# Another order for the seven steps of a nested product, and the plain product read by ScalarE alone

## The chip, the cores and the metric

The kernel runs on one core of one Trainium2 chip. The metric is the device time of one execution in microseconds (us), the median of three runs. All data are float32. TensorE runs a float32 matmul of this kernel as two passes, so one product in the code is two rows in the profile.

## The reference

Eight images x of 512 channels and 32 x 32 = 1024 positions go through two layers.

```python
# layer 0: attention with 8 heads of 64 channels, 1x1 convolutions
q, k, v = conv(x, Wq, bq), conv(x, Wk, bk), conv(x, Wv, bv)
attn = softmax(einsum('bhdn,bhdm->bhnm', q, k) * scale, axis=-1)
x = x + conv(einsum('bhnm,bhdm->bhdn', attn, v), Wp, bp)
# layer 1: non-local block, then a normalization over batch and positions
g_x, theta_x, phi_x = conv(x, g_w), conv(x, theta_w), conv(x, phi_w)   # 256 channels each
f = einsum('bcn,bdn->bcd', theta_x, phi_x) / n
z = conv(einsum('bcd,bdn->bcn', f, g_x), W_w) + x
out = (z - mean(z)) * rsqrt(var(z) + eps) * gamma + beta
```

The change touches the products for q, k and v of layer 0, a 512 x 512 weight times 512 x 1024 data for each image.

## The kernel before

The kernel takes the images one after the other. For image b it runs the attention (scores L578, exponential on ScalarE L581, weighted sum L604), then the products q, v and k of image b+1, then the projection of image b (L340, `pp`), theta and phi (`ptp`), g (`pg`), and the sum z. TensorE, VectorE (`dve`) and SyncE's DMAs are held in the order in which the program lists them.

Large products use a Strassen-Winograd scheme: seven products of quarter size and sums of quarters take the place of eight products. The seven steps are listed in `SEVEN`, each with its weight block, its data block, a chain number, and the quarter that is read out when it is done. Steps with one chain number accumulate in one place, and the sum so far is read out after each of them.

```python
SEVEN = (("11", 0, "11", 0, (("11", True),)), ("s1t1", 3, "t1", 1, (("22", True),)),
         ("s2t2", 4, "t2", 0, (("12", True),)), ("s4", 6, "22", 1, (("12", False),)),
         ("s3t3", 5, "t3", 0, (("22", False),)), ("12", 1, "21", 2, (("11", False),)),
         ("t4", 2, "t4", 0, (("21", True),)))
SIX = (((1, "21", "11"), (6, "22", "12")), ((3, "t1", "22"), (4, "t2", "T6")), ((5, "t3", "T7"), (2, "t4", "21")))
ORDER = (0, 1, 2, 5, 4, 3, 6)
```

For q, k and v of images 1 to 7 the function `six` is used, 21 times in all. Of the seven outer products, one (`plain()`) is done as it is: two halves into one accumulator tile each (L386 for q and k, L383 for v). Each half is read twice, into the temporary `T6` and into the quarter "11" of the result. The function `begin` makes these reads: three of the four by ScalarE (L510 for q and k, L545 for v), the fourth by VectorE (L508, L545). The other six outer products are nested: each is again seven steps. They are done in the three pairs of `SIX`, the two products of a pair side by side (m = 0 and 1), so that one step is two products. The results of a pair go to the quarters 11 and 12, then 22 and T6, then T7 and 21. `ORDER` is the order of the seven steps inside a pair.

A pair has four accumulator tiles from the ring of four tags s0 to s3 (`next_bank`). A tile has two halves of 512 columns. `slots[m]` and `slots[2 + m]` belong to product m. Which tile and half a step uses follows from its chain: chain 0 the first half of `slots[m]`; before the change, chain 1 the first half of `slots[2 + m]`, and chain 2 the second half of `slots[2 + m]`. So along `ORDER` the steps go to the two tiles of a product strictly in turn. The products are L418 (q, k) and L415 (v).

After each step its sum is read from the tile. The first read into a result quarter is a copy by ScalarE (L424), every later one an add by VectorE (L426). The quarters 11 and T6, which already hold the plain product, take adds only, and T7 has a read of its own (`third`: ScalarE L514 for q, VectorE L516 for k and L546 for v).

Between the steps VectorE has other work, which `fills` places. For q it makes the last sums of the next image's data: t4 (L252, from x) behind the plain product, and the four inner sums of t3 and of t4 (L264), one after each of some steps. Behind the second pair ("middle") come the softmax denominators (L644) and their reciprocal (L655).

Of the kernel before, what the change touches and what calls it, by code (L numbers as in the profile page):

```python
# [10 lines left out]
AF = mybir.ActivationFunctionType  # L11
ALU = mybir.AluOpType
# [18 lines left out]
def unshifted(ctx: ExitStack, tc: tile.TileContext, a: dict, out: bass.AP):  # L31
    nc = tc.nc
# [32 lines left out]
    dve = sp = pe  # L65
# [281 lines left out]
                between[n]()  # L347

    SIX = (((1, "21", "11"), (6, "22", "12")), ((3, "t1", "22"), (4, "t2", "T6")), ((5, "t3", "T7"), (2, "t4", "21")))
    ORDER = (0, 1, 2, 5, 4, 3, 6)  # L350

    def six(name, w, data, positions_out, at, begin, third, fills, by_scalar=False):

        fills = dict(fills)
        shape = [P, 4, 256] if positions_out else [P, 2, 512]
        temps = {}

        def to(q):
            if q[0] != "T":
                return at(q)  # L360
            if q not in temps:
                temps[q] = w3.tile(shape, F32, tag="acc", name=f"{q}_{name}")
            return temps[q]

        def piece(q, i, j):
            if positions_out:
                return to(q)[:, j * 2:j * 2 + 2, i * P:(i + 1) * P]
            return to(q)[:, i, j * 256:(j + 1) * 256]

        def add(q, of, engine=None):  # L370
            dve((engine or nc.gpsimd).tensor_tensor(to(q), to(q), to(of), ALU.add))

        def plain():
            d = data["11"]
            for half in range(2):
                ps = next_bank(f"{name}_0_{half}")[:, 0, :]
                if positions_out:
                    ps = ps.rearrange("p (i f) -> p i f", f=256)
                for i in range(2 if positions_out else 1):
                    for k in range(2):  # L380
                        if positions_out:
                            at = (half * 2 + i) * P
                            pe(nc.tensor.matmul(ps[:, i, :], d[:, k, at:at + P], w[:, 0, k, :],  # L383
                                                start=(k == 0 and i == 0), stop=(k == 1), skip_group_check=True))
                        else:
                            pe(nc.tensor.matmul(ps, w[:, 0, k, half * P:(half + 1) * P], d[:, k, :],  # L386
                                                start=(k == 0), stop=(k == 1), skip_group_check=True))
                for q in ("T6", "11"):
                    at_ = to(q)[:, half * 2:half * 2 + 2, :] if positions_out else to(q)[:, half, :]
                    begin(at_, ps, half, half and q == "11")  # L390
            load_w("first")

        plain()
        for one in fills.pop("plain", ()):
            one()
        for n, pair in enumerate(SIX):
            if n == 2:
                add("12", "22")
                add("12", "T6")
                for one in fills.pop("middle", ()):  # L400
                    one()
            slots = [next_bank(f"{name}_in_{n}_{i}") for i in range(4)]
            free[:] = [free[2], free[3], free[0], free[1]]
            begun = set()
            for step, which in enumerate(ORDER):
                _, wi, di, chain, reads = SEVEN[which]
                for m, (outer, of, q) in enumerate(pair):
                    a, d = w.inner(outer)[wi], data[f"inner {of}"][di]
                    ps = slots[m if not chain else 2 + m][:, chain // 2, :256]
                    start = (m, chain) not in begun  # L410
                    begun.add((m, chain))
                    if positions_out:
                        ps = ps.rearrange("p (i f) -> p i f", f=P)
                        for i in range(2):
                            pe(nc.tensor.matmul(ps[:, i, :], d[:, i * P:(i + 1) * P], a, start=start and not i, stop=True,  # L415
                                                skip_group_check=True))
                    else:
                        pe(nc.tensor.matmul(ps, a, d, start=start, stop=True, skip_group_check=True))  # L418
                    for (i, j), is_first in reads:
                        i, j = int(i) - 1, int(j) - 1  # L420
                        if is_first and q == "T7":
                            third(piece(q, i, j), ps, piece("T6", i, j), i)
                        elif is_first and q not in ("11", "T6"):
                            nc.scalar.copy(piece(q, i, j), ps)  # L424
                        else:
                            dve(nc.vector.tensor_tensor(piece(q, i, j), piece(q, i, j), ps, ALU.add))  # L426
                for one in fills.pop((n, step), ()):
                    one()
            load_w()
        assert not fills, fills  # L430
        if by_scalar:
            add("T7", "T6")
        add("22", "T7")
        add("21", "T7")
# [22 lines left out]
    for x_part, w_part in (((0, 1, 0), (w_first[0], 0, 0, 0, 1)), ((1, 2, 0), (w_first[0], 0, 0, 1, 2)),  # L457
# [5 lines left out]
        if w_part:  # L463
            to, m, k, c0, c1 = w_part
            nc.scalar.dma_start(to[:, c0:c1], quarter("WqT", m, k)[:, c0:c1])
    ps = next_bank("warm_ps")[:, 0, :]
# [34 lines left out]
    def heads_of(b, what, w, bias, data, pin=lambda ins: None, steps=None, fills=None, **how):  # L501

        t = mats.tile([P, CC, N], F32, tag=what, name=f"{what}_{b}")

        if fills is not None:
            def begin(to, ps, i, by_vector):
                if by_vector:
                    dve(nc.vector.tensor_scalar(to, ps, bias[:, i:i + 1], 1.0, ALU.add, ALU.mult))  # L508
                else:
                    nc.scalar.activation(to, ps, AF.Identity, bias=bias[:, i:i + 1])  # L510

            def third(to, ps, of, i):
                if what == "q":
                    nc.scalar.activation(to, ps, AF.Identity, bias=steps[:, i:i + 1])  # L514
                else:
                    dve(nc.vector.scalar_tensor_tensor(to, ps, steps[:, i:i + 1], of, ALU.add, ALU.add))  # L516

            six(f"p{what}_{b}", w, data, False, lambda q: t[:, rows(q), cols(q)], begin, third, fills,
                what == "q")
            return t  # L520

        def first(q, ps):
            for m in range(2):
                c = rows(q).start + m
                if how.get("early") and q == "21":
                    nc.vector.tensor_scalar(t[:, c, cols(q)], ps[:, m, :], bias[:, c:c + 1], 1.0, ALU.add, ALU.mult)
                else:
                    nc.scalar.activation(t[:, c, cols(q)], ps[:, m, :], AF.Identity, bias=bias[:, c:c + 1])

        seven(f"p{what}_{b}", w, data, False, first, add_to(t, pin), **how)  # L530

        return t

    def values(b, w, data, fills=None):
        v = mats.tile([P, NB, C], F32, tag="v", name=f"v_{b}")

        def at(q):
            return v[:, (int(q[1]) - 1) * NB // 2:int(q[1]) * NB // 2, (int(q[0]) - 1) * C // 2:int(q[0]) * C // 2]

        def as_v(ps):  # L540
            return ps.rearrange("p h (i f) -> p (h i) f", f=C // 2)

        if fills is not None:
            six(f"pv_{b}", w, data, True, at,
                lambda to, ps, _, by_vector: dve(nc.vector.tensor_copy(to, ps)) if by_vector else nc.scalar.copy(to, ps),  # L545
                lambda to, ps, of, _: dve(nc.vector.tensor_tensor(to, of, ps, ALU.add)), fills)  # L546
            return v
        seven(f"pv_{b}", w, data, True, lambda q, ps: nc.scalar.copy(at(q), as_v(ps)),
              lambda q, ps: dve(nc.vector.tensor_tensor(at(q), at(q), as_v(ps), ALU.add)))
        return v  # L550
# [436 lines left out]
    data = {"11": b11, "21": b21, "22": b22, "t1": t[0], "t2": t[1], "t3": t[2], "t4": t[3], "name": "x_0"}  # L987
    q = heads_of(0, "q", w, bq, data, dve, early=True, by_chunk=True)
# [19 lines left out]
    for b in range(B):  # L1008
# [41 lines left out]
        if not last:  # L1050
            data = nxt["data"]
            t3, t4 = (inner_one_by_one(data, of) for of in ("t3", "t4"))
            q = heads_of(b + 1, "q", weights("WqT"), bq, data, dve, steps=dq, fills={
                "plain": [lambda: more_sums(data, (4,), dve), t3[0]], (0, 0): t3[1:2], (0, 1): t3[2:3],
                (0, 2): t3[3:], (0, 6): t4[:1], (1, 0): t4[1:2], (1, 1): t4[2:3], (1, 2): t4[3:],
                "middle": [lambda: nxt.update(products=normalize(denominators(next_bank(f"den_{b}"))))]})
            products = nxt["products"]
            v = values(b + 1, weights("WvT"), data, fills={(0, 6): products[:2], (1, 6): products[2:]})
# [305 lines left out]
```

## Time and profile before

| | |
|---|---|
| three runs | 2135.11, 2135.65, 2136.66 us; median 2135.65 us |
| the profiled execution | 2135.05 us, span 2133.3 us, mean granted TensorE clock 0.996 |
| TensorE matmul busy | 2093.9 us (98% of the span) |
| VectorE, ScalarE, GpSimd busy | 1409.1, 781.1, 526.0 us |
| q stage of the image at 973.6 us | 25.43 us: PE 23.67, DVE 17.26, ACT 8.20 busy |
| v stage of that image | 22.55 us: PE 22.48, DVE 12.75, ACT 6.33 |
| k stage of that image | 22.09 us: PE 21.82, DVE 13.18, ACT 6.42 |

The stages are seven times in the program, for images 1 to 7. Matmuls are pipelined: a pass of 256 columns has a row of 379 ns, but the next pass starts 216 ns after it. A row of idle time therefore counts from the end of the row before, not from the time at which the next pass could have started. PE stands for the matmuls and PEld for the weight loads ahead of them.

### The profile page before, as it was taken

The numbers are of one execution on the slowest core, as the hardware profiler recorded it, in microseconds if no ns is written. First come the engines' busy times: TensorE is split into PE (matmuls) and PEld (weight loads), VectorE is DVE, ScalarE is ACT, GpSimd is POOL, SyncE is SP. The second block draws the span as 40 slices with busy tenths as digits, with TensorE's granted clock in tenths as the row PEclk, the third lists the DMA queues.
The fourth block names the chain that finished last, engine by engine and source line by source line (L and its number), as shares of the span: only waits on it lengthen the run. The fifth ranks groups of instructions, "written<-read, shape, count | busy, mean of one in ns | idle before, by whom it ended". The sixth has DMA issues, their size and how long they took to land.

```text
span 2133.3 us, 33255 instructions
## 1 busy us (share of the span) xinstructions
PE 2093.9 (98%) x13486; PEld 1173.4 (55%) x13486; DVE 1409.1 (66%) x2072; ACT 781.1 (37%) x1024; POOL 526.0 (25%) x392
## 2 busy tenths in 40 slices
PE   9999999999999999999999999999999999999995
PEld 4535863358733677336773377633775348743462
DVE  6587567765578655786557766577664775556736
ACT  1464204642046410563105631066312652056116
POOL 0012900128001370014601155011550118111000
PEclk9999999999999999999999999999999999999998
DMA  6253533244232432325324253142543235212768
GB/s 227 84 144 77 172 146 111 38 89 142 99 114 41 105 121 99 117 40 139 101 83 121 41 146 122 50 124 42 152 151 139 41 51 165 92 27 40 235 219 318
DMA packets 71728, 243.56 MB, mean 114 GB/s; under 512 B 12688, under 2 KB 21136, under 8 KB 69520
## 3 DMA queue, kind: packets, MB, share of 16 engines
q1 hardware_dynamic: 60640, 215.01, 30.3%
q0 software_dynamic: 9072, 24.78, 9.5%
q8 instruction: 108, 1.77, 0.3%
q10 hardware_dynamic: 1856, 1.56, 0.3%
q14 instruction: 52, 0.43, 0.1%
HBM read 160.45 MB, written 47.32 MB: 97 GB/s over the span
## 4 chain that ended last, share of the span: by engine, by line
PE 94%; DVE 2%; ACT 2%; DMA 1%; issue 0%; SPq 0%; DVEq 0%; ACTq 0%
PE ps L578 21%; PE po L604 21%; PE ptp L340 9%; PE pp L340 7%; PE pv_in L415 6%; PE pk_in L418 6%; PE pq_in L418 5%; PE pg L340 4%; PE pz L340 3%; PE pf L799 2%; PE pp_in_s L297 2%; PE pq L386 1%; PE pq L340 1%; PE pv L383 1%; PE pv L340 1%; PE pk L386 1%
## 5 line engine op out<-in xcount | busy, mean ns | idle before, releaser
L581 ACT ACTIVATE e<-ps 128x1024 f32<-128x1024 f32 x512 | 523.0, 1025 | 422.8 <-PE ps L578 412.1
L587 DVE TENSOR_TENSOR acc<-acc,e 128x1024 f32<-128x1024 f32 x384 | 469.9, 1224 | 103.6 <-ACT e L581 93.7
L578 PE MATMUL ps<-q,k 64*64 64x512 f32 x4096 | 529.3, 589 | 0.0
L604 PE MATMUL po<-e,v 64*64 64x512 f32 x4096 | 528.7, 589 | 0.0
L617 POOL DMA_DIRECT2D fold<-acc x189 | 144.8, 766 | 1359.1 <-DMA fold<-acc 650.4
L604 PEld LDWEIGHTS po<-e,v 64*64 64x64 f32 x4096 | 156.6, 133 | 282.9 <-issue 275.5
L578 PEld LDWEIGHTS ps<-q,k 64*64 64x64 f32 x4096 | 155.5, 133 | 283.4 <-issue 277.3
L842 ACT ACTIVATE g<-pg,gb 128x512 f32<-128x512 f32 x31 | 21.3, 688 | 442.0 <-PE pg L340 441.9
L585 DVE TENSOR_TENSOR acc<-e,e 128x1024 f32<-128x1024 f32 x64 | 78.3, 1224 | 120.8 <-ACT e L581 118.6
L340 PE MATMUL ptp<-w_tp,t_x 128*128 128x256 f32 x512 | 114.4, 379 | 0.0
L340 PEld LDWEIGHTS ptp<-w_tp,t_x 128*128 128x128 f32 x512 | 97.3, 190 | 13.2
L340 PE MATMUL pp<-t_o,w_WpT 128*128 128x512 f32 x208 | 100.8, 592 | 0.0
L340 PE MATMUL ptp<-w_tp,x 128*128 128x256 f32 x384 | 86.8, 379 | 0.0
L340 PEld LDWEIGHTS ptp<-w_tp,x 128*128 128x128 f32 x384 | 73.0, 190 | 13.3 <-issue 3.8
L340 PE MATMUL pp<-o,w_WpT 128*128 128x512 f32 x144 | 67.8, 593 | 1.9 <-DVE o L684 1.9
L424 ACT COPY v<-pv_in 128x256 f32<-128x256 f32 x84 | 31.3, 372 | 100.8 <-PE pv_in L415 33.1
L424 ACT COPY k<-pk_in 128x256 f32<-128x256 f32 x84 | 31.3, 373 | 97.2 <-PE pk_in L418 96.7
L684 POOL TENSOR_TENSOR o<-o,r 128x1024 f32<-128x1024 f32 x28 | 65.3, 2368 | 0.0
L770 DVE TENSOR_TENSOR tp<-tp,ptp 128x1024 f32<-128x1024 f32 x24 | 29.3, 1221 | 51.2 <-PE ptp L340 51.2
L737 DVE SCALAR_TENSOR_TENSOR x<-pp,bp,x 128x512 f32<-128x512 f32 x52 | 37.6, 746 | 35.0 <-PE pp L340 35.0
L418 PE MATMUL pq_in<-i_t_x,w_WqT 128*128 128x256 f32 x224 | 57.1, 382 | 2.9 <-DVE fold L655 2.9
L424 ACT COPY q<-pq_in 128x256 f32<-128x256 f32 x84 | 31.3, 373 | 76.3 <-PE pq_in L418 75.8
(233 smaller groups left out, 2942.1 us busy)
## 6 DMA issues: line engine op xcount, KB each, us to landing
fold<-acc POOLq DMA_DIRECT2D x189, 128.0 KB, 3.1
w_WqT<-kept_WqT SPq DMA_DIRECT2D x21, 896.0 KB, 4.6
w_WvT<-kept_WvT SPq DMA_DIRECT2D x21, 896.0 KB, 4.9
w_WkT<-kept_WkT SPq DMA_DIRECT2D x21, 896.0 KB, 5.3
r<-den_d SPq DMA_DIRECT2D x32, 512.0 KB, 6.9
x<-in_x_dram SPq DMA_DIRECT2D x30, 512.0 KB, 5.8
spill<-x SPq DMA_DIRECT2D x24, 512.0 KB, 4.0
z<-spill SPq DMA_DIRECT2D x24, 512.0 KB, 10.1
```

The costliest lines, as they stand in the source:

```text
L297: pe(nc.tensor.matmul(ps, a[wi], d[di], start=s not in begun, stop=True, skip_group_check=True))
L340: pe(nc.tensor.matmul(to_ps, lhsT(k), rhs(k), start=(s, at) not in begun, stop=(k == nk - 1), skip_group_check=True))
L415: pe(nc.tensor.matmul(ps[:, i, :], d[:, i * P:(i + 1) * P], a, start=start and not i, stop=True, skip_group_check=True))
L418: pe(nc.tensor.matmul(ps, a, d, start=start, stop=True, skip_group_check=True))
L424: nc.scalar.copy(piece(q, i, j), ps)
L578: pe(nc.tensor.matmul(ps[c * P // 2:(c + 1) * P // 2, j, :], k[r, p, keys], q[r, p, h * 512:(h + 1) * 512], start=True, stop=True, skip_gr ...
L581: nc.scalar.activation(e, ps, AF.Exp, scale=SCALE)
L585: nc.vector.tensor_tensor(accs[u], es[u, 0], e, ALU.add)
L587: ins = nc.vector.tensor_tensor(accs[u], accs[u], e, ALU.add)
L604: pe(nc.tensor.matmul(ps[j * D:(j + 1) * D, r, :], v[keys, m, (2 * p + j) * D:(2 * p + j + 1) * D], e[keys, j, :], start=(m == 0), stop=(m ...
L617: nc.gpsimd.dma_start(to, part_of, accum_op=ALU.add)
L684: dve((engine or nc.vector).tensor_tensor(at, at, of, ALU.mult))
```

## The change

There are three parts. First, the order of the seven steps becomes 0, 5, 1, 2, 4, 3, 6, and chain 2 (step 5 alone) moves from the second half of `slots[2 + m]` to the second half of `slots[m]`, the tile of chain 0. Second, the fourth read of the plain product goes from VectorE to ScalarE, so that ScalarE makes all four, in q, k and v. Third, the four inner sums of t3 go, with t4, ahead of everything that VectorE does for the first pair of q, and those of t4 are spread over other steps.

```diff
-    ORDER = (0, 1, 2, 5, 4, 3, 6)
+    ORDER = (0, 5, 1, 2, 4, 3, 6)
...
-                    begin(at_, ps, half, half and q == "11")
+                    begin(at_, ps, half)
...
-                    ps = slots[m if not chain else 2 + m][:, chain // 2, :256]
+                    ps = slots[2 + m if chain == 1 else m][:, chain // 2, :256]
...
-            def begin(to, ps, i, by_vector):
-                if by_vector:
-                    dve(nc.vector.tensor_scalar(to, ps, bias[:, i:i + 1], 1.0, ALU.add, ALU.mult))
-                else:
-                    nc.scalar.activation(to, ps, AF.Identity, bias=bias[:, i:i + 1])
+            def begin(to, ps, i):
+                nc.scalar.activation(to, ps, AF.Identity, bias=bias[:, i:i + 1])
...
-                lambda to, ps, _, by_vector: dve(nc.vector.tensor_copy(to, ps)) if by_vector else nc.scalar.copy(to, ps),
+                lambda to, ps, _: nc.scalar.copy(to, ps),
...
-                "plain": [lambda: more_sums(data, (4,), dve), t3[0]], (0, 0): t3[1:2], (0, 1): t3[2:3],
-                (0, 2): t3[3:], (0, 6): t4[:1], (1, 0): t4[1:2], (1, 1): t4[2:3], (1, 2): t4[3:],
+                "plain": [lambda: more_sums(data, (4,), dve), *t3],
+                (0, 2): t4[:1], (0, 3): t4[1:2], (0, 6): t4[2:3], (1, 0): t4[3:],
```

## The prediction

> **What bounds the kernel.** I read the page first, then TensorE's waits, then the timeline of one image.
>
> ```profile
> span 2133.3 us, 33255 instructions
> ...
> PE 2093.9 (98%) x13486; PEld 1173.4 (55%) x13486; DVE 1409.1 (66%) x2072; ACT 781.1 (37%) x1024; POOL 526.0 (25%) x392
> ...
> PEclk9999999999999999999999999999999999999998
> ```
>
> TensorE is busy for 98% of the span at full clock. The change neither adds nor removes a matmul, so it acts only through the time that TensorE stands still in the 21 calls of `six`. TensorE's waits, in total, count and longest, are there:
>
> ```profile
> PE pq_in L418 <- DVE q L426: 7.7, 7, 1.1
> PE pq_in L418 <- DVE fold L655: 2.9, 7, 0.6
> PE pk_in L418 <- DVE k L508: 1.9, 7, 0.3
> PE pq_in L418 <- DVE q L508: 1.9, 7, 0.3
> ```
>
> Each comes once per image. The timeline of the q stage at 973.6 us shows the first and the last of them:
>
> ```profile
> 978.07 0.75 DVE L508 TENSOR_SCALAR q<-pq,bq 128x512 f32<-128x512 f32 x1 [3.02 <-ACT T_pq L510]
> ...
> 978.87 0.30 PEld L418 LDWEIGHTS pq_in<-i_x,w_WqT 128*128 128x128 f32 x2 [0.67 <-DVE q L508]
> 978.87 0.70 PE L418 MATMUL pq_in<-i_x,w_WqT 128*128 128x256 f32 x2 [0.27 <-DVE q L508]
> ...
> 980.20 0.41 DVE L426 TENSOR_TENSOR q<-q,pq_in 128x256 f32<-128x256 f32 x1
> ...
> 980.67 1.13 PE L418 MATMUL pq_in<-i_x,w_WqT 128*128 128x256 f32 x4 [1.10 <-DVE q L426]
> ```
>
> VectorE stands idle for 3.02 us until ScalarE has read the second plain half, then reads that half itself, makes t4 (1.22) and one inner sum, and only then adds the first product of the pair. TensorE needs that tile again and waits 1.10 us. Two prices follow. From the end of a read to the weight load that it holds up it is 0.055 us (980.617 to 980.672). The weight load, normally hidden under the matmul before, then stands in the open: the matmul's row is 483 ns long instead of 379, so 0.104 us more.
>
> ```profile
> L418 PE MATMUL pk_in<-i_x,w_WkT x112: 379/379/483, 240.9 to 1803.4; 128*128 128x256 f32 x112
> ```
>
> A row ends 0.163 us after its successor could start (379 less 216 ns). So the true loss of a wait is its idle time plus 0.163 plus 0.104, that is idle plus 0.27.
>
> **What goes.** Per image: 1.10 + 0.27 = 1.37 (L426), 0.27 + 0.27 = 0.54 (L508, q), 0.39 + 0.27 = 0.65 (reciprocal L655, in the image at 973.6), 0.54 (L508, k), and 0.33 in v, where one product came 0.06 us late with the weight load in the open. Sum: 3.4 us. All of it should go. VectorE no longer holds the fourth plain read. t4 and the inner sums of t3 take 1.13 + 4 x 0.34 = 2.5 us (each starts that long after the one before it, in the rows above and those of L264 between them) from 975.05, where the last add of the attention ends, so they end at 977.6, before the first sum can be read at 977.78. The reciprocal's bank is needed one step (0.86 us) later, and it was 0.65 late. The inner sums of t4 fit in VectorE's gaps in pairs 0 and 1. The 21 reads that ScalarE takes over cost it 21 x 0.6 us beside TensorE, except for what is charged below.
>
> **What comes.** In the old order the steps of a product take its two tiles in turn: 0 | 1 | 0 | 2 | 0 | 1 | 0 by chains, where 1 and 2 share a tile. In the new order the tiles are A A B A A B A. Twice in each pair a step follows directly on a step in the same tile: 5 after 0, and 4 after 2. The waits in the built program say that this counts: the product of step 5 waits for the read of step 0's product in that tile, by VectorE (m = 0) or ScalarE (m = 1), although it goes to the other half; and 4 waits for the read of 2. The old program also has such waits by whole tile, but with a step between them, so no row of before shows one costing time. What the interval is worth is seen in an undisturbed step:
>
> ```profile
> 995.58 1.03 PE L418 MATMUL pq_in<-t_x,w_WqT 128*128 128x256 f32 x4
> ...
> 996.21 0.42 DVE L426 TENSOR_TENSOR T_pq<-T_pq,pq_in 128x256 f32<-128x256 f32 x1 [2.09 <-PE pq_in L418]
> 996.23 0.84 PEld L418 LDWEIGHTS pq_in<-i_t_x,w_WqT 128*128 128x128 f32 x4
> 996.44 1.03 PE L418 MATMUL pq_in<-i_t_x,w_WqT 128*128 128x256 f32 x4
> ```
>
> A step is four passes, 0.863 us (995.58 to 996.44). The first product's read starts 0.63 after its first pass and lasts 0.42. In the same tile the next step's first matmul can start at 0.63 + 0.42 + 0.055 + 0.104 = 1.21, so 0.35 late. The second product runs 0.43 later throughout and adds nothing, unless its read is the longer one or is held up. Other readers:
>
> ```profile
> L424 ACT COPY q<-pq_in 128x256 f32<-128x256 f32 x84 | 31.3, 373 | 76.3 <-PE pq_in L418 75.8
> L514 ACT ACTIVATE T_pq<-pq_in,dq 128x256 f32<-128x256 f32 x28 | 13.3, 474 | 31.3 <-PE pq_in L418 30.5
> ...
> L516 DVE SCALAR_TENSOR_TENSOR T_pk<-pk_in,dk,T_pk 128x256 f32<-128x256 f32 x28 | 13.5, 484 | 5.4 <-PE pk_in L418 4.8
> ```
>
> The same sum with 0.37 gives 0.30 late, with 0.47 gives 0.40, with 0.48 gives 0.41. In v a step is eight passes of 0.1115, 0.89 us, and the late part is 0.33 for VectorE's 0.42.
>
> Each pair has two such places. In pair 0 (quarters 11 and 12) VectorE reads m = 0, which makes 2 x 0.35 in q and k and 2 x 0.33 in v. At the first place of q and k the fourth plain read is in the way too: it starts 0.59 after the third (977.35), at 977.93, frees ScalarE at 978.52, so the copy of m = 1 ends at 978.89 and its tile is free at 979.05; with the 0.35 the product was due at 978.79. That adds 0.26, and 0.03 in v by the same steps. The sums for q, k and v are 0.96, 0.96 and 0.69. In pair 1 (22 and T6) m = 0 is late by 0.30 for ScalarE's copy, and m = 1 brings it to 0.35 for VectorE's add; two places make 0.70 in q and k, 0.66 in v. In pair 2 (T7 and 21) it is 2 x 0.40 in q, 2 x 0.41 in k and 2 x 0.33 in v.
>
> q 2.46, k 2.48, v 2.01: 7.0 us per image. Less the 3.4 that goes: +3.6 us per image, times 7 images, +25 us. TensorE sets the stages behind (projection, theta, scores), so nothing there gives it back. On the profiled execution that is 2135.05 + 25 = 2160; on the median, 0.6 higher, I say 2161 us.
>
> Bounds of the price: were the weight load hidden after all, 18 x 0.104 x 7 = 13 us less, 2148. Should every third read queue behind another VectorE operation (0.33, the spacing of its adds), 6 x 0.33 x 7 = 14 more, 2175. I stay in the middle because every wait of before, worked out this way, gives its row.
>
> No row of before has a step directly behind another in its tile, so the wait of 5 for 0 rests on the built program. [...]
>
> The 1.10 us waits of before left PEclk at 9. [...]
>
> **Rivals.** *The reads are in time* (faster, 0.03): only the 3.4 us go, 7 x 3.4 = 24, 2112 us. It decides if a read has ended 0.70 us after its product's start (0.863 less 0.16); above it ends at 1.05. *Half the places cost nothing* (same, 0.03): if step 5 does not lose time on step 0, nine places of 0.35 are 3.2 against 3.4, about 2135 us. *Reads queue up* (slower, 0.06): up to 2175, as above; against it, VectorE is busy for 17.26 of the 25.43 us of the q stage and for less of v and k. *The clock drops* (slower, 0.03): the mean of 0.996 stands for 8.5 us lost in the whole span, and only the last slice of PEclk is an 8; a like loss in each of 7 images would give 2161 + 60 = 2221. It would decide if a wait of some tenths of a microsecond in every third of a pair counted for the clock more than the one of 1.10 us did.
>
> **The numbers.** The forecast itself has 0.85 and a range of 2155 to 2167 (0.05 us on each of 18 places, 0.9 us per image, 6 us in all). For 8 in 10 with part of the bounds on the price: 2153 to 2169. A measurement of this kernel tells 0.2%, 4.3 us, from no change. Faster 0.03, same 0.03, slower 0.94.
>
> **What would show it.** Right: TensorE's waits list new entries under pq_in, pv_in and pk_in for L426, L424, L514 (new number L511) and L516, about 18 per image, each with the 483 ns rows; idle of 0.03 to 0.14 us each, since 0.27 of each loss is not idle in the rows; the old L426 and reciprocal waits gone; the image's stages 73.7 us instead of 70.07. Wrong: stages at or under 70 us, or a step 5 that starts 0.86 after step 0.

## The result, and the profile after

The changed kernel takes 2163.28 us (2161.63 to 2164.71 in four runs) against 2135.79 us for the kernel before in the same comparison: 1.0128 times as long, with an interval of 1.0111 to 1.0146. The prediction was 2161 us, with 2153 to 2169 as its range and 0.94 for slower.

The profiled execution took 2162.94 us, its span 2161.2, at a mean granted clock of 0.995. The code of after is a few lines shorter, so lines move: the plain reads are L507 (q, k) and L542 (v), ScalarE's and VectorE's reads in `third` are L511 (q), L513 (k) and L543 (v), the reciprocal is L652, and o of the last image is L681. L414 to L426 keep their numbers. The head of the page:

```profile
span 2161.2 us, 33290 instructions
...
PE 2124.8 (98%) x13486; PEld 1168.8 (54%) x13486; DVE 1402.0 (65%) x2051; ACT 790.3 (37%) x1045; POOL 526.3 (24%) x392
...
PEclk9999999999999999999999999999999999999998
```

TensorE has the same 13486 matmuls, but is "busy" for 30.9 us longer (2124.8 against 2093.9), while the span grew by 27.9. VectorE has 21 instructions fewer and ScalarE 21 more, which is the fourth plain read. So the loss isn't where a reader looks first, in idle time of TensorE; it is inside rows that became longer, and in later starts that lie under the end of the row ahead. TensorE's waits after (total, count, longest; the list shows none under 0.15 us) list only little:

```profile
PE pp L340 <- DVE o L681: 2.1, 1, 2.1
PE pk_in L418 <- DVE T_pk L513: 1.5, 7, 0.2
PE warm_ps L468 <- DVE folds L483: 1.1, 1, 1.1
PE pk_in L418 <- DVE k L426: 1.1, 7, 0.2
PE pq_in L418 <- DVE q L426: 0.8, 5, 0.2
...
```

Under `six` that is 3.4 us, where before had 14.4. The waits of the weight loads show what took their place:

```profile
PEld pq_in L418 <- ACT q L424: 8.2, 21, 0.4
PEld pk_in L418 <- ACT k L424: 8.2, 21, 0.4
PEld pk_in L418 <- DVE T_pk L513: 8.1, 14, 0.6
PEld pq_in L418 <- ACT T_pq L511: 7.5, 14, 0.5
PEld pq_in L418 <- DVE q L426: 7.2, 14, 0.6
...
PEld pv_in L415 <- DVE v L426: 4.1, 14, 0.3
```

Counts of 14 and 21 are two and three in each image, where before had seven of one kind, one in each. Each is some tenths of a microsecond long, and most of it lies beside the end of the matmul ahead, so that TensorE itself shows little idle time. The matmul that waits is lengthened by its own weight load (shortest, median and longest row in ns):

```profile
L418 PE MATMUL pq_in<-x,w_WqT x84: 379/379/483, 190.8 to 1777.4; 128*128 128x256 f32 x84
```

The first pair of q in the image at 984.6 us shows both places of the new order, 5 behind 0 and 4 behind 2 (timeline: start, duration, engine, line; in brackets the idle time ahead and what ended it):

```profile
988.16 1.03 PE L418 MATMUL pq_in<-x,w_WqT 128*128 128x256 f32 x4
...
988.86 0.42 DVE L426 TENSOR_TENSOR q<-q,pq_in 128x256 f32<-128x256 f32 x1 [0.20 <-PE pq_in L418]
988.95 0.68 ACT L507 ACTIVATE q<-pq,bq 128x512 f32<-128x512 f32 x1
...
989.34 0.30 PEld L418 LDWEIGHTS pq_in<-x,w_WqT 128*128 128x128 f32 x2 [0.55 <-DVE q L426]
989.34 1.30 PE L418 MATMUL pq_in<-x,w_WqT 128*128 128x256 f32 x4 [0.15 <-DVE q L426]
989.52 0.38 ACT L424 COPY q<-pq_in 128x256 f32<-128x256 f32 x1
989.94 0.30 PEld L418 LDWEIGHTS pq_in<-x,w_WqT 128*128 128x128 f32 x2 [0.31 <-ACT q L424]
...
992.45 0.30 PEld L418 LDWEIGHTS pq_in<-i_x,w_WqT 128*128 128x128 f32 x2 [0.48 <-DVE q L426]
```

Step 0 starts at 988.16; VectorE reads its first product until 989.28; only then does the weight load of step 5 start, at 989.34. Due 0.863 us behind 988.16, step 5 starts its first pass 0.104 us (the weight load in the open) behind 989.34, so it is 0.42 late, with only 0.15 of that as idle time of PE. The second product is held up by ScalarE's copy, which had to let the fourth plain read (988.95) go first. The old waits are gone: VectorE no longer reads a plain half here, and the reciprocal in the third pair, which held up TensorE before, now ends after 1.76 us without anything of `six` waiting for it:

```profile
1003.12 1.76 DVE L652 RECIPROCAL fold<-den 128x256 f32<-128x256 f32 x1 [0.61 <-PE den L641]
...
1004.24 0.73 PEld L418 LDWEIGHTS pq_in<-t_x,w_WqT 128*128 128x128 f32 x4 [0.53 <-ACT T_pq L511]
```

By stage (window, its length, then busy time of PE, PEld, DVE, ACT, POOL, the granted clock, the DMA share and GB/s), q, v and k of that image:

```profile
984.62:1009.93 25.31, 24.75 (x113) 17.14 (x110) 17.15 (x37) 8.64 (x20) 7.01 (x5) 1.00 0.48 121
1009.93:1034.27 24.34, 23.90 (x185) 22.34 (x184) 12.29 (x30) 6.71 (x17) 21.01 (x9) 1.00 0.69 196
1034.27:1058.44 24.17, 23.52 (x95) 16.71 (x93) 12.63 (x31) 6.89 (x16) 23.60 (x16) 1.00 0.29 93
```

The clock is 1.00 in all three. The time without a matmul row (length less PE busy) is 1.65 us in these three windows, spread over 18 short spells, against 2.10 us in five spells before: it fell while the stages grew. q is 0.12 us shorter than before, v 1.80 and k 2.07 longer. In images 2 to 7 the three together take 73.81 us against 70.06, in image 1 74.92 against 71.33: 6 x 3.75 + 3.6 = 26.1 of the 27.9 us. Between the stages nothing moved (191.33 us from one to the next for most images, and each such stretch the same in both kernels). The rest, 1.9 us, is behind the last stage, and is taken up in the last section.

### The profile page after: what moved, and what is told of

Read it like the earlier page. It is cut to its first block, busy times and chain, and to the rows that moved or that the text cites. A ratio compares the mean times of both kernels' runs of the same rounds, so it can differ in the third digit from the quotient of the medians.

```text
span 2161.2 us, 33290 instructions
## 1 busy us (share of the span) xinstructions
PE 2124.8 (98%) x13486; PEld 1168.8 (54%) x13486; DVE 1402.0 (65%) x2051; ACT 790.3 (37%) x1045; POOL 526.3 (24%) x392
## 4 chain that ended last, share of the span: by engine, by line
PE 94%; DVE 2%; ACT 2%; issue 1%; DMA 1%; DVEq 0%; SPq 0%; ACTq 0%
PE ps L575 20%; PE po L601 20%; PE ptp L340 9%; PE pp L340 7%; PE pv_in L415 6%; PE pq_in L418 6%; PE pk_in L418 6%; PE pg L340 4%; PE pz L340 3%; PE pf L796 2%; PE pp_in_s L297 2%; PE pq L386 1%; PE pq L340 1%; PE pv L383 1%; PE pv L340 1%; PE pk L386 1%
## 5 line engine op out<-in xcount | busy, mean ns | idle before, releaser
L340 PE MATMUL ptp<-w_tp,t_x 128*128 128x256 f32 x512 | 114.4, 379 | 0.0
L340 PEld LDWEIGHTS ptp<-w_tp,t_x 128*128 128x128 f32 x512 | 97.3, 190 | 13.2
L340 PE MATMUL pp<-t_o,w_WpT 128*128 128x512 f32 x208 | 100.8, 592 | 0.0
L340 PE MATMUL ptp<-w_tp,x 128*128 128x256 f32 x384 | 86.8, 379 | 0.0
L426 DVE TENSOR_TENSOR v<-v,pv_in 128x256 f32<-128x256 f32 x112 | 46.6, 422 | 53.9 <-PE pv_in L415 50.6
L340 PEld LDWEIGHTS ptp<-w_tp,x 128*128 128x128 f32 x384 | 73.0, 190 | 13.3 <-issue 3.8
L426 DVE TENSOR_TENSOR k<-k,pk_in 128x256 f32<-128x256 f32 x112 | 46.8, 421 | 49.0 <-PE pk_in L418 47.0
L340 PE MATMUL pp<-o,w_WpT 128*128 128x512 f32 x144 | 69.4, 605 | 2.1 <-DVE o L681 2.1
L681 POOL TENSOR_TENSOR o<-o,r 128x1024 f32<-128x1024 f32 x28 | 65.2, 2368 | 0.0
```

What stands on the lines that cost most here:

```text
L340: pe(nc.tensor.matmul(to_ps, lhsT(k), rhs(k), start=(s, at) not in begun, stop=(k == nk - 1), skip_group_check=True))
L681: dve((engine or nc.vector).tensor_tensor(at, at, of, ALU.mult))
```

## The experiments

Two theories stand against each other. By the prediction's, the time is lost at the places where a step follows another in its tile, some 0.4 us at each, and the read by ScalarE alone is a gain that hides part of it. By the rival, it is lost by what the change moves on VectorE and ScalarE (the fourth read, the early sums), or by the other sequence of the steps as such, and the shared tile costs little. A place is a step that directly follows another in its tile. A stage is the time from the first plain product of q to the first product of the projection; its times are those of images 2 to 7 in the profiled execution. Run times are medians of four runs with their range, and the bracket behind a ratio is its 95% interval. The names e1 to g1 are used again further down.

**The order alone, on the kernel before (e1).**

```diff
-    ORDER = (0, 1, 2, 5, 4, 3, 6)
+    ORDER = (0, 5, 1, 2, 4, 3, 6)
...
-                    ps = slots[m if not chain else 2 + m][:, chain // 2, :256]
+                    ps = slots[2 + m if chain == 1 else m][:, chain // 2, :256]
```

> The new order and the new place of chain 2 alone; the fourth plain read stays with VectorE and the early sums of x stay where they were. One image's stage (first plain product of q to first product of the projection) was 70.06 us before and 73.81 after; without any loss on TensorE it would be 66.6. Theory (a step directly behind a step in the same tile waits for that step's read): the 18 places per image cost what they cost after, and the first of each stage costs more, since VectorE's plain read and the sums stand ahead of the read that step 5 now waits for: about 10.7 us of loss, a stage of 77.4 us, 2187 us in all. Rival 1 (the loss comes from ScalarE, which has four plain reads ahead of its copies): about the time of before, 2136 us, or less. Rival 2 (5 behind 0 costs nothing, since it goes to the other half): 4 behind 2 alone, a stage of 70 us, 2136 us.

Measured: 2194.02 us (2191.32 to 2196.90), 1.0269 [1.0252, 1.0287] of before. The stage takes 77.44 us in images 2, 3 and 5 as worked out, but 78.8 to 79.1 in images 4, 6 and 7. TensorE's waits show what the old order had hidden:

```profile
PE pq_in L418 <- DVE q L426: 17.5, 7, 2.5
PE pk_in L418 <- DVE k L426: 7.2, 7, 1.0
PE pv_in L415 <- DVE v L426: 5.9, 7, 0.8
```

With step 5 directly behind step 0, TensorE waits 2.5 us in every q for the first add of the pair, which on VectorE is queued behind the fourth plain read, t4 and an inner sum. Before, the same add came 1.10 us too late; a step of 0.86 us in the other tile no longer lies ahead of the wait, nor the 0.54 us by which that step was itself held up: 1.10 + 0.86 + 0.54 = 2.50. The order by itself costs more than the whole change does. The 7 us above the expectation are those three images (in image 4 the granted clock was 0.50 for a while, last section), and the part behind the last stage, 320.79 us instead of 317.54, with a wait of 3.41 us for o and 5.40 us for the eight passes behind it, which before took 3.70. The mean granted clock of the span is 0.993, against 0.996 before.

**The change with the old order (e2).** The converse: after, with both lines above undone.

> The other two parts alone: all four plain reads on ScalarE and the early sums, in the old order and the old tiles, where no step follows another in its tile. Theory: the waits for VectorE's plain read go, what stays per image is 0.65 (reciprocal), 0.34 in q and in k (the fourth read on ScalarE frees its tile late) and 0.1 in v: 1.4 us of loss, a stage of 68.1 us, 2122 us in all. Rival 1 (ScalarE's four reads make the loss): well above before, toward 2163 us.

Measured: 2121.95 us (2121.61 to 2122.28), 0.9934 [0.9918, 0.9951]; stage 68.05 us. This is faster than before by 14 us, which is 7 times the 2.0 us by which the stage became shorter. Of TensorE's waits in `six` one is left, the reciprocal:

```profile
PE pq_in L418 <- DVE fold L652: 2.9, 7, 0.6
```

**The new steps, tiles in turn (e3).** After, with step 5 second as in the change, but with an order that goes to the two tiles in turn (A B A B A B A).

```diff
-    ORDER = (0, 5, 1, 2, 4, 3, 6)
+    ORDER = (0, 5, 2, 1, 4, 3, 6)
...
-                    ps = slots[2 + m if chain == 1 else m][:, chain // 2, :256]
+                    ps = slots[m if not chain else 2 + m][:, chain // 2, :256]
```

> The order 0, 5, 2, 1, 4, 3, 6 with chain 2 in its old tile: step 5 comes second as after the change, but the tiles alternate as before. The other two parts as after. Theory: no place of the same tile, so as with the old order: a stage of 68.1 us, 2122 us. Rival 3 (it is the early step 5 as such that costs, its add on VectorE into a quarter just written): near 2163 us.

Measured: 2121.68 us (2121.44 to 2122.79), 0.9934 [0.9917, 0.9950]; stage 68.05 us, the same as with the old order (q, v and k of image 4, columns as above):

```profile
967.80:991.65 23.85, 23.40 (x113) 17.75 (x110) 16.75 (x37) 8.63 (x20) 7.01 (x5) 1.00 0.47 127
991.65:1013.95 22.30, 22.30 (x186) 21.87 (x184) 12.20 (x30) 6.72 (x17) 20.98 (x9) 1.00 0.73 215
1013.95:1035.84 21.89, 21.83 (x94) 17.40 (x93) 12.45 (x31) 6.89 (x16) 21.40 (x15) 1.00 0.31 103
```

Against the old order the steps 1 and 5 have changed places, and it makes no difference. So it isn't the early step 5 that costs, but two steps in one tile one after the other.

**Four places instead of two (e5).** As the last one, but with an order whose tiles are A A B B B A A.

```diff
-    ORDER = (0, 5, 1, 2, 4, 3, 6)
+    ORDER = (0, 2, 1, 5, 3, 4, 6)
...
-                    ps = slots[2 + m if chain == 1 else m][:, chain // 2, :256]
+                    ps = slots[m if not chain else 2 + m][:, chain // 2, :256]
```

> The order 0, 2, 1, 5, 3, 4, 6 with chain 2 in its old tile, the other two parts as after: four places per pair instead of two (2 behind 0, 5 behind 1, 3 behind 5, 6 behind 4), none of them 5 behind 0 or 4 behind 2. Theory: 36 places per image at 0.30 to 0.41, 13.7 us of loss with the fourth read's share, a stage of 80.4 us, 2208 us. Rival 3 (only the early step 5 costs) gives 2122 us. Rival 2 (only places in the same half cost): three of these four places are in the same half or follow one, so 5 behind 1 and 3 behind 5 are free and about 2165 us come out.

Measured: 2207.72 us (2207.21 to 2210.75), 1.034 [1.0323, 1.0357]; stage 80.29 us, but 80.64 in images 4 and 7, where one read of v came late. Image 4:

```profile
1003.83:1031.30 27.47, 26.40 (x112) 16.17 (x109) 17.29 (x37) 8.65 (x20) 7.01 (x5) 1.00 0.47 118
1031.30:1058.14 26.84, 25.84 (x186) 22.95 (x184) 12.40 (x30) 6.72 (x17) 20.99 (x9) 1.00 0.58 171
1058.14:1084.47 26.33, 25.17 (x95) 15.76 (x94) 12.80 (x31) 6.88 (x16) 24.17 (x16) 1.00 0.25 85
```

With none, 18 and 36 places in an image the stage takes 68.05, 73.81 and 80.29 us. It is a dose: twice the places, about twice the time. Of the four places two are in the same half of the tile (2 behind 0, 6 behind 4) and two go to the other half (5 behind 1, 3 behind 5). In the first pair of q of image 4 those to the other half are 0.42 and 0.35 us late, 6 behind 4 is 0.35 late. So the other half is no protection, which settles rival 2.

**The new order with the old tiles (f1).** After, with only the tile of chain 2 undone: A B B A A B A, again two places in a pair, at other steps.

```diff
-                    ps = slots[2 + m if chain == 1 else m][:, chain // 2, :256]
+                    ps = slots[m if not chain else 2 + m][:, chain // 2, :256]
```

> As after, but chain 2 stays in the second half of its old tile, so along 0, 5, 1, 2, 4, 3, 6 the tiles run A B B A A B A: again two places per pair, 1 behind 5 in place of 5 behind 0, and the second tile is needed one step earlier. Theory: 18 places as after, and the waits that the late use of the second tile had removed come back (0.65 behind the reciprocal, 0.34 in q and in k, 0.1 in v, partly inside the places): 8.2 us of loss per image, a stage of 74.9 us, 2169.5 us in all. Rival (the half or the place of step 5 in the tile of step 0 makes the loss): 2136 us or less.

Measured: 2172.96 us (2171.85 to 2174.78), 1.0176 [1.0159, 1.0193]; stage 75.13 us. Against the version with tiles in turn (e3) only the steps 1 and 2 have changed places, with the same tile for each step: that makes two places in a pair, 18 in an image, and 7.1 us. Moving chain 2 into the tile of chain 0 did not add a place: it moved one. What it saves against this version is seen in the waits, of which after has the second not at all and the first only as 0.8 us in all:

```profile
PE pq_in L418 <- DVE q L426: 3.5, 14, 0.5
PE pq_in L418 <- DVE fold L652: 2.9, 7, 0.6
```

**The fourth plain read back on VectorE (f2).** After, with the old `begin`.

```diff
-            def begin(to, ps, i):
-                nc.scalar.activation(to, ps, AF.Identity, bias=bias[:, i:i + 1])
+            def begin(to, ps, i, by_vector):
+                if by_vector:
+                    dve(nc.vector.tensor_scalar(to, ps, bias[:, i:i + 1], 1.0, ALU.add, ALU.mult))
+                else:
+                    nc.scalar.activation(to, ps, AF.Identity, bias=bias[:, i:i + 1])
...
```

> As after, but the fourth plain read is VectorE's again. VectorE then waits for ScalarE's third read, and makes that read, t4 and the four inner sums before the first add that step 5 waits for. Theory: 3.9 us at the first place of q, 1.1 in v, 1.3 in k, the rest as after: 11.8 us per image, a stage of 78.4 us, 2194.5 us, and more if TensorE's clock halves after the wait of 3.6 us, as it did for 3.4 us in three images of the run with the order alone (1.65 us each): up to 7 x 1.7 = 12 more, 2194 to 2206. Rival (ScalarE's four reads make the loss): below after.

Measured: 2204.50 us (2204.34 to 2205.84), 1.0323 [1.0306, 1.0341]; stage 78.52 us in image 4 and 79.9 to 81.2 in the others; the mean granted clock of the span is 0.991, against 0.996 before.

```profile
PE pq_in L418 <- DVE q L426: 25.4, 7, 3.6
```

The read by ScalarE is what makes the early sums and the new order bearable: without it the wait is 3.6 us, longer than the 2.5 us of the order alone (e1), because all four inner sums of t3 now lie ahead of the add too. In image 4 that is 4.7 us of the stage, in all seven images, with the lower clock, 41 us of the kernel: so much the ScalarE read is worth beside this order and the early sums.

**The early sums taken back (f3).** After, with the two lines of `fills` as before.

> As after, but the sums of x stay where they were before (one inner sum of t3 ahead, the rest between the steps). Theory: with the plain read gone from VectorE the sums fit between its adds, only the second place of the first pair of q is 0.05 later: a stage of 73.85 us, 2163.5 us, no difference to after that can be measured. Rival (the early sums carry a part of the gain): 2 us or more per image slower than after, 2177.

Measured: 2162.32 us (2162.00 to 2166.05), 1.0129 [1.0112, 1.0146]; stage 73.85 us. Against 73.81 that is 0.04 us per image, 0.3 us in all, which no run can tell. With ScalarE making all four reads, the early sums bring nothing beside the new order; beside the old order they were not tried alone.

**What is left, taken away (g1).** On top of the version with tiles in turn: the denominators are copied out of their bank before the reciprocal, so that the bank is free earlier; and the plain product is read into T6 alone, twice instead of four times, quarter 11 taking its first sum from T6.

```diff
-            dve(nc.vector.reciprocal(ri, den))
+            dve(nc.vector.tensor_copy(ri, den))
+            dve(nc.vector.reciprocal(ri, ri))
...
-                for q in ("T6", "11"):
-                    at_ = to(q)[:, half * 2:half * 2 + 2, :] if positions_out else to(q)[:, half, :]
-                    begin(at_, ps, half)
+                at_ = to("T6")[:, half * 2:half * 2 + 2, :] if positions_out else to("T6")[:, half, :]
+                begin(at_, ps, half)
...
-                            dve(nc.vector.tensor_tensor(piece(q, i, j), piece(q, i, j), ps, ALU.add))
+                            of = "T6" if is_first and q == "11" else q
+                            dve(nc.vector.tensor_tensor(piece(q, i, j), piece(of, i, j), ps, ALU.add))
```

> Order 0, 5, 2, 1, 4, 3, 6 with chain 2 in its old tile (no step behind another in its tile), the early sums as after, and two waits taken away: the denominators are copied out of their accumulator (0.42) before the reciprocal, and the quarter 11 is not set from the plain product any more: its first add takes T6, which holds the same values, so each half of the plain product is read once. Theory: of the 3.4 us per image of before 0.15 stays: a stage of 66.8 us, 2135.8 - 7 x 3.27 = 2113 us. Rival (something else bounds the stages once TensorE waits less, VectorE's adds for example): no better than the 2122 us of the alternating order.

Measured: 2112.58 us (2111.92 to 2113.29), 0.989 [0.9873, 0.9906]; stage 66.73 us. It beats both kernels, by 23 us the one before. The two waits were taken away together, so what each is worth is not shown. TensorE's waits have nothing of `six` left, and in the three stages (columns as above) TensorE is busy for the whole of the window:

```profile
PE pp L340 <- DVE o L682: 2.1, 1, 2.1
PE warm_ps L468 <- DVE folds L483: 1.1, 1, 1.1
PE den L641 <- ACT got L238: 0.3, 1, 0.3
```

```profile
964.71:987.67 22.96, 22.96 (x113) 17.84 (x109) 17.06 (x38) 7.62 (x18) 7.01 (x5) 1.00 0.47 125
987.67:1009.88 22.21, 22.21 (x186) 21.80 (x184) 12.19 (x30) 5.84 (x15) 20.96 (x9) 1.00 0.76 222
1009.88:1031.45 21.57, 21.57 (x95) 17.49 (x94) 12.44 (x31) 5.84 (x14) 21.08 (x15) 1.00 0.32 105
```

This is taken as the floor of the stage with these matmuls. In q one weight load of the third pair still comes some 0.1 us late, so there the floor is a little high. It makes the loss of each version readable without any model of pipelined rows: 70.06 - 66.73 = 3.3 us in an image before (3.4 by the prediction), 7.08 after.

## Why the prediction was right

**What goes.** All of it went, as worked out. With the old order (e2) only 68.05 - 66.73 = 1.3 us of the 3.4 is left, half of it the reciprocal's 0.65. So the fourth read and the early sums together are worth 2.0 us in an image beside the old order. The step by which the new place of step 5 gives the reciprocal time is right too: its wait is in the versions with the old tiles (e2, e3, f1) and not in after. The prediction let the early sums share in the gain ("ahead of the first sum"); f3 shows that beside the new order there was nothing to share, since with ScalarE reading all four VectorE has that time anyway; that the 2.0 us of e2 are the read's alone is likely, but not shown.

**What comes.** The floor gives a test of each product by itself:

| us per image | predicted loss | after | floor (g1) | measured loss |
|---|---|---|---|---|
| q | 2.46 | 25.30 | 22.96 | 2.34 |
| v | 2.01 | 24.34 | 22.21 | 2.13 |
| k | 2.48 | 24.17 | 21.57 | 2.60 |
| sum | 7.0 | 73.81 | 66.73 | 7.08 |

Place by place in the image at 984.6 us, from start to start of the steps, those of pairs 1 and 2 in q are late by 0.35 and 0.40 as worked out. The first place of pair 0, in q and in k, makes 0.42 and 0.17 behind it, 0.59 where 0.35 + 0.26 were set down: the fourth plain read on ScalarE is charged rightly. Some terms were too small: in v the first places of pairs 0 and 2 are 0.40 late against 0.36 and 0.33, in k those of pairs 1 and 2 are 0.42 and 0.48 late against 0.35 and 0.41. In the table q comes out 0.12 too low (the floor there is some 0.1 high) and v and k 0.12 each too high, so that 7.0 against 7.08 is closer than the single terms are. Net, the prediction has +3.6 and the traces +3.75 us, which over seven images is 1 us.

**The signs.** Those named came, but one not where it was looked for: TensorE's own list has 19 entries in the whole run and none under `pv_in`, since most of the idle spells are under 0.15 us; the 18 per image show in the waits of the weight loads.

**The price per place** is 7.08 / 18 = 0.39 us with two places in a pair and (80.29 - 66.73) / 36 = 0.38 with four. So the reads do not queue up, not even with twice as many, save for one read of v in two images of e5 (the rival with 2175 us is out), and the weight load does stand in the open, in rows of 483 ns (the low bound of 2148 is out).

**The rivals.** That half the places cost nothing would have had step 5 start 0.86 us behind step 0; it starts 1.28 behind it, counted past its weight load. The weight load of step 5 waits for the read of the other half (0.55 us, `DVE q L426`, in the timeline above), and that is a wait that the program makes by whole tile. Whether the chip would bear step 5 without it was not tried: that needs a tile for each half, and the attention reads both halves as one. For these orders the question need not be answered: with the tiles in turn no place is left and none costs (e3).

That the clock drops for many short waits is ruled out for this spacing by the three rows of windows above: 18 delays of 0.3 to 0.6 us in 74 us, and the granted clock is 1.00; with 36 of them (e5) the mean of the span is still 0.996.

**What was not in the sum.** Between the two profiled executions the span grew by 27.9 us where the sum has 25. One of the 2.9 us is that of the under-sized terms; the other 1.9 lie behind the last stage, where no term stood.

## What to carry to other kernels

When steps share accumulator tiles, write down the tile of each step in its order: two steps in the same tile one behind the other cost here the whole way from the first matmul to the end of its read and the weight load, less the length of one step (0.4 us of a 0.86 us step), while one step in another tile between them hid it (e2, e3: a stage of 68.05 us against 73.81), unless the read itself was held up as in the kernel before. Here that loss hardly showed as idle time of the matmuls; look for weight loads that wait, and for matmul rows that are longer than their like. And try the parts of a change one by one: here the reads and sums together are worth -14 us, the order with its tiles +41 beside them, and the slower sum hid a gain of 0.7% (e2, e3), from which the two further edits of g1 make 1.1% against the kernel before.

## What was not expected of the hardware

Before, the granted clock is 0.60 in the last 23 us, in which TensorE has 1.82 us of matmuls. Elsewhere it fell to 0.50 behind waits of TensorE of 2.50 us (e1, image 4) and 2.09 us (after), and not behind others as long. The same wait of 2.5 us in two images of the version with the order alone (columns as above; the first two rows are image 2, the others image 4):

```profile
462.40:465.70 3.30, 0.91 (x5) 0.45 (x3) 2.50 (x5) 1.06 (x2) 0.77 (x1) 1.00 0.54 119
465.80:469.10 3.30, 3.17 (x13) 2.49 (x14) 2.46 (x7) 0.74 (x2) 0.77 (x1) 1.00 0.38 38
999.90:1003.30 3.40, 0.96 (x5) 0.51 (x3) 2.54 (x5) 1.06 (x2) 0.77 (x1) 1.00 0.50 119
1003.40:1006.70 3.30, 3.30 (x8) 2.68 (x9) 1.80 (x6) 0.00 (x0) 0.77 (x1) 0.50 0.36 36
```

Behind the wait TensorE does 13 passes in image 2 and 8 in image 4, which makes that stage 1.65 us longer. Images 4, 6 and 7 of the seven have the longer stage.

The wait for o in the last image's projection is in all ten kernels, so it can be set beside the time of the eight passes behind it (`pp<-o`, L340):

| kernel | wait for o, us | eight passes behind it, us |
|---|---|---|
| f3 | 1.55 | 3.70 |
| e5 | 1.65 | 3.70 |
| f1 | 1.80 | 3.70 |
| before | 1.86 | 3.70 |
| e2 | 2.01 | 3.70 |
| after | 2.09 | 5.38 |
| g1 | 2.12 | 3.70 |
| e3 | 2.26 | 3.70 |
| f2 | 2.81 | 3.70 |
| e1 | 3.41 | 5.40 |

So the length of the wait alone does not decide: behind 2.09 us the passes are slow, behind 2.12, 2.26 and 2.81 us they are not. In f2, too, the wait in q is 3.6 us in each of the seven images (25.4 in all), and the stage is 1.4 to 2.7 us shorter in image 4 than in images 2, 3 and 5 to 7. What decides is open.

The changed kernel has one such stretch, behind the wait of 2.09 us in the table:

```profile
2032.40:2035.70 3.30, 3.02 (x4) 1.48 (x5) 3.27 (x4) 0.00 (x0) 0.00 (x0) 0.54 1.03 408
2035.80:2039.20 3.40, 3.40 (x9) 1.35 (x8) 3.30 (x5) 0.00 (x0) 0.00 (x0) 0.96 1.03 404
```

From 2032.69 to 2036.09 us the clock is 0.50, and in the 3.4 us ahead of it and behind it 1.00. The span behind the last stage is 319.42 us, against 317.54 before and 317.78 to 318.00 in three versions whose eight passes there took 3.70 us (e2, f3, g1). So 1.4 to 1.9 us of the profiled execution of after belong to none of its parts as such: with longer waits at the same point, of 2.26 (tiles in turn) and 2.81 us (fourth read on VectorE), the passes behind were not slower.
